# Four graph layers on one core: the head of the last layer reordered, and two small reorderings in its skip LSTMs

## The chip, the cores and the metric

The kernel runs on one core of one Trainium2 chip. The metric is the time of one execution on the device in microseconds (us), and the median of the runs is compared. The core has five engines, each with its own in-order instruction queue: TensorE (PE, matmuls; its weight loads are shown apart as PEld), VectorE (DVE), ScalarE (ACT), GpSimd (POOL), and SyncE (SP), which here only starts DMA transfers. An instruction waits at the head of its queue until the semaphores that it names have been reached, and all behind it wait too.

## What is computed

The input `x` is 128 sequences of 64 positions with 256 features; a graph of 64 nodes connects the positions. Four layers follow each other, each of the form `x = layernorm(x + layer(x))`. The change lies wholly in the last one:

```
h = relu(adj @ (x @ Wg0 + bg0))
h = relu(adj @ (h @ Wg1 + bg1))
for p in 1..4:                       # skip LSTMs
    nw = 64 // p                     # windows of p positions
    last = LSTM_p(windows of h)      # p steps, gates i, f, g, o; zero start; last hidden state
    h[:, p-1, 2p-1, ...] = last      # written over the last position of each window
x = layernorm(x + h)
```

All of it is in float32. The third layer ends with a batch norm over all rows, so nothing of the last layer's input exists before the third layer is complete.

## The kernel before

**Blocks, groups, pairs.** The rows are cut into 16 blocks of 512 (8 sequences). Two blocks make a group of 16 sequences, two groups a pair. There are four pairs, and the LSTMs run pair after pair (`lstm(pair)`), with both groups of a pair side by side in tiles such as `H[:, group, k]`, the input of the LSTMs (features on the partitions, `k` or `m` is the half of the 256 features).

**The graph convolutions, `gcn`.** It is a generator, one block each, and is advanced one step at a time. For the first four blocks the steps are:

1. start two loads of the residual `x2r` (L964); scale the third layer's result by the batch norm (four ACT operations, L970);
2. and 3. for each half `a`: four PE transposes (L988), then `norm`: the residual sum (L994), statistics (L95, L96, L85, L98) on DVE, the power and the normalisation on POOL (L86, L100), and two stores of the result (L999);
4. `neighbours`: the 64 small matmuls with the graph (L953), whose two result banks are copied into `hT` or `xs` by DVE (L1019) and ACT (L1020);
5. and 6. the first weight matrix for each half `m` of the features (L1026), the bias on DVE (L1028), the relu on ACT (L1030);
7. and 8. the second weight matrix for each half `a` of the rows (L1038), its bias on DVE (L1041);
9. `neighbours` again, and the relu into `H` by DVE (L1049) and ACT (L1050).

Blocks 0 and 2 take their PSUM banks from the pool `g` (two banks), blocks 1 and 3 from the pool `l` (six banks), which the LSTMs use as well. Blocks 0 and 1 fill group 0 of pair 0 and blocks 2 and 3 group 1.

**The head of the layer.** Before the LSTMs of pair 0 can start, blocks 0 and 1 must be through. A list of block numbers written out by hand, `for n in [0, 0, 0, 1, 1, 1, ...]`, says in which order the steps of the four blocks are issued; the steps that are left of blocks 2 and 3 are put beside the first units of the LSTMs with `put(pair, part, unit, ...)`.

**What fixes the order.** Each step is recorded through `given`, which puts it behind the latest recorded instruction of every engine. So the order of the list is the order of every engine's queue; within one step a scheduler may still move independent instructions past each other.

**The LSTMs.** For p=1 a window is one position: `gates` issues the three gates of a quarter (L1075, six matmuls of 512 columns per unit), and DVE writes the result back into `H` (L1086). For p=2 to 4 the first step of the windows has no hidden state: `plain` issues its gates from `H` (L1183), with two groups `g` and two halves `k` for each half `m`. Later steps (`Gate`, L1218) use seven products in place of eight. After the last step of a window, `output` writes `o * tanh(c)` (L1148) in four parts, one for each half `m` and group, back into `H`, from which the next p starts; for p=4 it writes into `lasts` instead (tile `hd`, L1139). The write of half 0 of group 0 comes first, those of half 1 of group 1, half 0 of group 1 and half 1 of group 0 follow.

**The end.** The last thing in the program is `final` of the last two groups with `pieces=2`, group 1 ahead of group 0: `hd` is transposed on PE (L1363), added to the residual (L1364), normalised, and stored (L1368).

Of the kernel before, what the change touches and what calls it, by code (L numbers as in the profile page):

```python
# [34 lines left out]
SKIP = 4  # L35
# [6 lines left out]
def kernel(ctx: ExitStack, tc: tile.TileContext, i, out):  # L42
# [72 lines left out]
    with ExitStack() as two:  # L115
# [598 lines left out]
        def hidden(q, m):  # L714
            return Z[q][:, m, :] if m < 2 else Aq(q)[:, (m - 2) * QT:(m - 1) * QT]
# [16 lines left out]
        def put(q, m, p_):  # L732
            nc.scalar.activation(hidden(q, m), p_, AF.Identity, bias=b1[:, m:m + 1])
# [112 lines left out]
    def lbank(shape):  # L846
        return ps.tile([P] + shape, F32, name="l", bufs=6)
# [4 lines left out]
    def given(do, *args):  # L852
        traced = nc.cur_bb.bb.instructions
        first = len(traced)
        with ExitStack() as order:
            for e in latest.values():
                order.enter_context(tc.issue_after(e))
            r = do(*args)
        for t in traced[first:]:
            if t.engine in (mybir.EngineType.PE, mybir.EngineType.DVE, mybir.EngineType.Activation,  # L860
                            mybir.EngineType.Pool):
                latest[t.engine] = t
        return r
# [189 lines left out]
    def gate_of(n):  # L1053
        return "ifgo".index(n), AF.Tanh if n == "g" else AF.Sigmoid

    def lstm(pair):
# [36 lines left out]
        for p in range(2, SKIP + 1):  # L1093
# [9 lines left out]
            def inp(r, s, m):  # L1103

                w0 = runs[r][0] * p
                return H[:, :, m, w0:w0 + nw * p, :].rearrange("p n (w s) b -> p n w s b", s=p)[:, :, :, s, :]

            def rows():
                return [late.tile([P, 2, nw, GB], F32, name="gate", bufs=6) for m in range(2)]
# [21 lines left out]
            def output(r, s, m, o, t, groups):  # L1131

                last = s == p - 1
                if last and p == SKIP:
                    for n in groups:

                        if (pair * 2 + n) not in lasts:
                            lasts[pair * 2 + n] = late.tile([P, 2, KD, P], F32, name="hd", bufs=3)
                        nc.vector.tensor_mul(lasts[pair * 2 + n][:, :, m],  # L1139
                                             *(v[m][:, n].rearrange("p (c w) b -> p c (w b)", c=2) for v in (o, t)))  # L1140
                    return

                dst = inp(r, s, m) if last else hid[:, m]
                if len(groups) == 2:
                    nc.vector.tensor_mul(dst, o[m], t[m])  # L1145
                else:
                    n = groups[0]
                    nc.vector.tensor_mul(dst[:, n], o[m][:, n], t[m][:, n])  # L1148

            def bias_of(n, m):  # L1150
                at, f = gate_of(n)
                return f, bias[:, p - 1, 2 * at + m:2 * at + m + 1]
# [15 lines left out]
            def tanh(n, tiles, m):  # L1168
                if n == "i":
                    nc.scalar.activation(tiles["g"][m], cell[:, m], AF.Tanh)  # L1170

            def plain(n, r, tiles):

                t = tiles[n] = rows()
                at, _ = gate_of(n)
                for m in (1, 0):
                    f, b = bias_of(n, m)
                    joint = 2 * nw * GB <= QT
                    banks = lbank([2, nw, GB]) if joint else None
                    for g in (1, 0):  # L1180
                        one = banks[:, g] if joint else lbank([nw, GB])
                        for k in range(KD):
                            nc.tensor.matmul(one, w.raw[0][:, k, at, m, :], inp(r, 0, k)[:, g],  # L1183
                                             start=k == 0, stop=k == KD - 1)
                        if not joint:
                            nc.scalar.activation(t[m][:, g], one, f, bias=b)
                    if joint:
                        nc.scalar.activation(t[m], banks, f, bias=b)
                for m in (1, 0):
                    finish(n, r, 0, tiles, m)  # L1190
                    tanh(n, tiles, m)
# [69 lines left out]
            for r in range(len(runs)):  # L1261
                if p > 2:
                    yield "gap", unit
                for s in range(p):
                    last = s == p - 1
                    if s == 0:
                        tiles = {}
                        for at, n in enumerate("gio"):
                            if at == 0 and p > 2:
                                given(input_sums, r, 1)  # L1270
                            given(plain, n, r, tiles)
                            if at == 0 and p == 2:
                                given(input_sums, r, 1)
                            if at < 2:
                                yield "at", unit
                                unit += 1
                    else:
                        names = "fgio"
                        for at, n in enumerate(names):
                            G = nxt or Gate(n, r, s, tiles)  # L1280
                            nxt = None
                            G.product(1)
                            G.product(5)
                            if prev:
                                prev.act(1)
                                prev.act(0)
                                prev.after(1)
                                G.product(2)
                                prev.after(0)
                                prev.tanh(1)  # L1290
                            G.product(6)
                            if n == "o":
                                G.act(0, 0)
                            if prev:
                                prev.tanh(0)
                            G.product(7)
                            if at == 0:
                                given(input_sums, r, s + 1)
                                G.product(3)
                                G.product(2)  # L1300
                                G.product(4)
                            elif at < 3:
                                G.product(4)
                                G.product(3)
                            if at < 3:
                                yield "at", unit
                                unit += 1
                            prev = G
                        o = prev
                        prev = None  # L1310
                        o.act(1, 1)
                        o.product(3)
                        o.act(0, 1)
                        o.product(4)
                        o.act(1, 0)
                        given(output, r, s, 0, o.tiles["o"], o.tiles["g"], (0,))

                    if not last:
                        tiles = {}
                        nxt = Gate("f", r, s + 1, tiles)  # L1320
                        for j in (1, 5, 6, 7, 3, 2):
                            given(nxt.part, j, 0)
                    elif p < SKIP:
                        yield "wait", unit + 1
                    if s:
                        given(output, r, s, 1, o.tiles["o"], o.tiles["g"], (1,))
                        given(output, r, s, 0, o.tiles["o"], o.tiles["g"], (1,))
                        given(hidden_sums, s, lambda: output(r, s, 1, o.tiles["o"], o.tiles["g"], (0,)))
                    else:
                        given(hidden_sums, s, lambda: None)  # L1330
                    yield "at", unit
                    unit += 1
                    if not last:
                        yield "gap", unit
# [38 lines left out]

    parts = [gcn(n // 2, n % 2, gbank if n % 2 == 0 else lbank, "hT" if n % 2 == 0 else "xs") for n in range(4)]
    first = [prepare(weights_of[0, p]) for p in (2, 3)]
    for n in [0, 0, 0, 1, 1, 1, 0, 1, 0, 1, 2, 0, 1, 2, 0, 1, 3, 2, 0, 1, 0, 1, 3, 2, 3]:
        given(next, parts[n])
    for part in first:
        next(part)
# [7 lines left out]
            kind, u = key if isinstance(key, tuple) else ("at", key)  # L1387
            side.setdefault((pair, kind, u), []).append(part)

    put(0, parts[2], 0, 0, 1, 1)  # L1390
    put(0, parts[3], 0, 1, 1, 2, 2)
    put(0, parts[2], 2)
    put(0, parts[3], 2)
    put(0, first[0], 3, 4)
    put(0, first[1], 9, 11)

# [6 lines left out]
    for k in range(NP):  # L1403
# [5 lines left out]
        for n in range(2):  # L1409
            g = k * 2 + n  # L1410
            for s in range(SKIP - 1):
                u = 34 + 4 * s + 2 * n
# [59 lines left out]
```

## Time and profile before

| | |
|---|---|
| median of 3 runs | 2073.12 us (2072.30, 2073.12, 2073.14) |
| the profiled execution | 2071.63 us, of which 2069.8 us are the span of the engines' records |
| granted TensorE clock over the span | 0.985 |
| PE busy | 1970.3 us (95%) in 11619 matmul passes |
| DVE / ACT / POOL busy | 56% / 46% / 35% |
| the last layer | from about 773 us to the end |

A float32 matmul stands in the records as two passes. A line of the chain or of the timeline gives the start in us, the length, the engine, the program's line, the operation, `output<-inputs`, the shape and a count. In brackets stands how long the engine had been idle before it and what ended that. A row of the windows view gives, for one stretch, the busy time of each engine, the granted clock of PE as a share of full speed, and the busy share of the DMA engines.

### The profile page before, as it was taken

To read this page: it belongs to the slowest core of one execution; us is meant where nothing else is said; L and a number is where in the kernel's file an instruction comes from. 1 tells how busy PE (TensorE), PEld (TensorE's weight loads), DVE (VectorE), ACT (ScalarE), POOL (GpSimd) and SP (SyncE) were. 2 spreads that over 40 slices of the span, in tenths; PEclk is the share of its full clock that TensorE was granted. 3 is DMA by queue.
4 is the path that set the end of the run, shared out by engine and by line. 5 is a ranking of instruction groups with operands and counts; after the bars stand their busy time and mean duration, and the time that the engine had idled before them with its cause. 6 is when DMAs were issued, how large, how long until landed. Compare 5 with 4: busy or idle time off the path is not lost.

```text
span 2069.8 us, 31352 instructions
## 1 busy us (share of the span) xinstructions
PE 1970.3 (95%) x11619; PEld 1379.4 (67%) x11619; DVE 1161.1 (56%) x2643; ACT 955.8 (46%) x1835; POOL 720.2 (35%) x890
## 2 busy tenths in 40 slices
PE   5999999998899999999999999999999999999997
PEld 4666667675454446587688587678587678586675
DVE  7456665554544446564566664566674466443556
ACT  2766666665337403543333643333644343533333
POOL 1123343343210004363445253245253245133354
PEclk9999999999999999999999999999999999999999
DMA  5354343332201128351232622032521031301012
GB/s 143 69 69 66 74 78 54 55 54 44 45 32 19 41 86 282 96 178 51 93 132 69 202 91 87 11 138 64 195 73 77 1 128 62 127 1 77 1 61 72
DMA packets 235961, 170.68 MB, mean 82 GB/s; under 512 B 150560, under 2 KB 213536, under 8 KB 232480
## 3 DMA queue, kind: packets, MB, share of 16 engines
q1 hardware_dynamic: 233952, 166.72, 28.8%
q8 instruction: 91, 1.49, 0.3%
q0 software_dynamic: 1024, 1.05, 0.2%
q10 hardware_dynamic: 832, 0.92, 0.1%
q14 instruction: 62, 0.51, 0.1%
HBM read 107.82 MB, written 60.82 MB: 81 GB/s over the span
## 4 chain that ended last, share of the span: by engine, by line
PE 75%; DVE 14%; ACT 4%; POOL 3%; issue 3%; DMA 1%; SPq 0%; DVEq 0%; POOLq 0%; ACTq 0%
PE l L1218 26%; PE l L1183 9%; PE l L1075 8%; PE pz L789 5%; PE pz L727 5%; PE e L331 3%; PE m L303 3%; PE g L1038 2%; PE m L238 2%; PE m L306 2%; PE z L340 2%; PE m L421 1%; DVE cell L1162 1%; PE g L953 1%; DVE ln_st L95 1%
## 5 line engine op out<-in xcount | busy, mean ns | idle before, releaser
L1218 PE MATMUL l<-xs,wx 128*128 128x256 f32 (+1 forms) x896 | 276.8, 399 | 5.1 <-DVE gate L1237 4.1
L1218 PE MATMUL l<-hs,wh 128*128 128x256 f32 (+1 forms) x896 | 275.1, 399 | 3.1 <-DVE hs L1112 3.1
L1233 ACT ACTIVATE kept<-l 128x256 f32<-128x256 f32 (+1 forms) x224 | 88.4, 402 | 340.0 <-PE l L1218 338.8
L86 POOL TENSOR_TENSOR ln_rs<-ln_rs,mhalf 128x2 f32<-128x2 f32 (+2 forms) x98 | 83.3, 850 | 454.0 <-DVE ln_rs L98 442.6
L1218 PE MATMUL l<-H,wx 128*128 128x256 f32 (+1 forms) x672 | 210.2, 401 | 3.4 <-DVE gate L1246 3.4
L1218 PE MATMUL l<-hid,wh 128*128 128x256 f32 (+1 forms) x672 | 208.8, 399 | 0.0
L1218 PEld LDWEIGHTS l<-xs,wx 128*128 128x128 f32 x896 | 168.8, 190 | 49.4 <-POOL st L100 5.1
L1218 PEld LDWEIGHTS l<-hs,wh 128*128 128x128 f32 x896 | 169.3, 190 | 45.5 <-DVE hs L1112 5.7
L1183 PE MATMUL l<-H,wx 128*128 128x256 f32 (+1 forms) x768 | 190.0, 407 | 10.1 <-DVE H L1148 10.1
L1251 ACT ACTIVATE gate<-gate,bias 128x512 f32<-128x512 f32 (+1 forms) x280 | 170.1, 656 | 35.2 <-DVE gate L1242 31.0
L1183 PEld LDWEIGHTS l<-H,wx 128*128 128x128 f32 x768 | 148.5, 195 | 51.7 <-DVE H L1148 16.0
L1075 PE MATMUL l<-H,wih 128*128 128x512 f32 x384 | 166.1, 593 | 0.0
L342 ACT ACTIVATE u<-z 128x1024 f32<-128x1024 f32 x128 | 130.3, 1025 | 64.2 <-PE z L340 63.4
L1218 PEld LDWEIGHTS l<-H,wx 128*128 128x128 f32 x672 | 126.0, 190 | 38.4 <-DVE gate L1246 7.4
L1218 PEld LDWEIGHTS l<-hid,wh 128*128 128x128 f32 x672 | 127.2, 190 | 32.0 <-issue 2.6
L1075 PEld LDWEIGHTS l<-H,wih 128*128 128x128 f32 x384 | 72.7, 190 | 89.3 <-issue 83.0
L1241 POOL TENSOR_TENSOR gate<-gate,kept 128x256 f32<-128x256 f32 (+1 forms) x84 | 65.0, 774 | 159.2 <-DVE kept L1239 159.2
L314 DVE TENSOR_TENSOR qs<-m,qs 64x256 fp32r<-64x256 f32 x128 | 54.0, 422 | 109.5 <-ACT qs L313 107.3
L727 PE MATMUL pz<-A,w 128*128 128x512 f32 x256 | 113.1, 595 | 0.0
L340 PE MATMUL z<-gath_r,qs 128*128 128x512 f32 x256 | 100.5, 480 | 0.6 <-ACT u L342 0.4
L1116 POOL TENSOR_TENSOR hs<-hid 128x256 f32<-128x256 f32 (+1 forms) x28 | 25.8, 921 | 207.0 <-DVE hid L1145 123.3
L1170 ACT ACTIVATE gate<-cell 128x512 f32<-128x512 f32 (+1 forms) x88 | 58.6, 666 | 82.4 <-DVE cell L1162 58.8
(277 smaller groups left out, 3629.2 us busy)
## 6 DMA issues: line engine op xcount, KB each, us to landing
wx<-sums SPq DMA_DIRECT2D x9, 2048.0 KB
wh<-sums SPq DMA_DIRECT2D x9, 1792.0 KB
way<-st SPq DMA_DIRECT2D x54, 256.0 KB
st<-way SPq DMA_DIRECT2D x216, 64.0 KB
xin<-in_x SPq DMA_DIRECT2D x16, 512.0 KB
ld<-table SPq DMA_DIRECT2D x16, 512.0 KB
x_dram<-y SPq DMA_DIRECT2D x16, 512.0 KB
x2r<-x_dram SPq DMA_DIRECT2D x32, 256.0 KB
```

The lines of the kernel that those rows point to most:

```text
L86: nc.gpsimd.tensor_tensor(dst, dst, mhalf[:, :n], OP.pow)
L303: nc.tensor.matmul(pq, xT[:, k, c * P:(c + 1) * P], wq[:, k, :], start=k == 0, stop=k == KD - 1)
L340: nc.tensor.matmul(z[:, k, :], L1[q]["qs"][c][:, s, k * P:(k + 1) * P], gath_r, start=True, stop=True)
L342: nc.scalar.activation(u, z, AF.Relu)
L727: nc.tensor.matmul(p_, w1[:, k, m * P:(m + 1) * P], Aq(q)[:, k * QT:(k + 1) * QT], start=k == 0, stop=k == KD - 1)
L789: nc.tensor.matmul(p_, w2[:, k, m * P:(m + 1) * P], hidden(q, k), start=k == 0, stop=k == M1 - 1)
L1075: nc.tensor.matmul(b, wih1[:, k, mw * P:(mw + 1) * P], Hw[:, k], start=k == 0, stop=k == KD - 1)
L1183: nc.tensor.matmul(one, w.raw[0][:, k, at, m, :], inp(r, 0, k)[:, g], start=k == 0, stop=k == KD - 1)
L1218: nc.tensor.matmul(self.banks[j], lhs, rhs, start=src == 0, stop=src == 1)
L1233: nc.scalar.activation(self.keep(j), b, AF.Copy)
L1241: e.tensor_tensor(t[0][:, 1], t[0][:, 1], k[5], OP.add)
L1251: given(lambda: nc.scalar.activation(dst, dst, f, bias=b))
```

## The change

There are three edits:

- **The head's list is another one, and so are the steps put beside the LSTM's first units.** The first weight matrix of block 0 is now issued between the transposes and norms of block 1, and block 0's second matrix beside block 1's first. Both norms of block 2 stand ahead of block 1's last step; block 2's first `neighbours` has left the head for unit 0 of the LSTMs. Beside the units, the remaining steps of blocks 2 and 3 take turns.
- **In `plain` group 0 is issued ahead of group 1.**
- **For the last step of p=4 alone, the four writes into `hd` come in another order:** half 1 of group 1 is moved up, ahead of the last gate's product 4 and so of its DVE sum (L1244), and half 0 of group 0 is moved behind half 0 of group 1.

```diff
--- before.py
+++ after.py
@@ plain @@
-                    for g in (1, 0):
+                    for g in range(2):
                         one = banks[:, g] if joint else lbank([nw, GB])
@@ last step of a window @@
                         o.act(0, 1)
+                        if p == SKIP and last:
+                            given(output, r, s, 1, o.tiles["o"], o.tiles["g"], (1,))
                         o.product(4)
                         o.act(1, 0)
-                        given(output, r, s, 0, o.tiles["o"], o.tiles["g"], (0,))
+                        if p < SKIP or not last:
+                            given(output, r, s, 0, o.tiles["o"], o.tiles["g"], (0,))
...
                     if s:
-                        given(output, r, s, 1, o.tiles["o"], o.tiles["g"], (1,))
+                        if p < SKIP or not last:
+                            given(output, r, s, 1, o.tiles["o"], o.tiles["g"], (1,))
                         given(output, r, s, 0, o.tiles["o"], o.tiles["g"], (1,))
+                        if p == SKIP and last:
+                            given(output, r, s, 0, o.tiles["o"], o.tiles["g"], (0,))
                         given(hidden_sums, s, lambda: output(r, s, 1, o.tiles["o"], o.tiles["g"], (0,)))
@@ head @@
-    for n in [0, 0, 0, 1, 1, 1, 0, 1, 0, 1, 2, 0, 1, 2, 0, 1, 3, 2, 0, 1, 0, 1, 3, 2, 3]:
+    for n in [0, 0, 0, 1, 0, 1, 0, 1, 0, 1, 0, 1, 2, 0, 1, 0, 1, 3, 1, 2, 2, 1, 3, 3]:
         given(next, parts[n])
...
-    put(0, parts[2], 0, 0, 1, 1)
-    put(0, parts[3], 0, 1, 1, 2, 2)
-    put(0, parts[2], 2)
-    put(0, parts[3], 2)
+    for n, u in [(2, 0), (3, 0), (2, 1), (2, 1), (3, 1), (3, 1), (2, 2), (2, 2), (3, 2), (3, 2), (2, 2), (3, 2)]:
+        put(0, parts[n], u)
```

The number of instructions on each engine stays the same. The order of POOL's queue does not change at all. On SP's queue seven transfers at the head trade places: block 2's second residual load and a load of `wh` go ahead of block 1's stores, two loads of `z` for later blocks and two residual loads of `final` go ahead of block 2's stores, and a third load of `z` goes behind the two stores of the weight sums.

## The prediction

> **What bounds the kernel now.** I read the page first, then the chain of waits, then the timeline and windows of the three places that are edited.
>
> ```profile
> PE 1970.3 (95%) x11619; PEld 1379.4 (67%) x11619; DVE 1161.1 (56%) x2643; ACT 955.8 (46%) x1835; POOL 720.2 (35%) x890
> L1183 PE MATMUL l<-H,wx 128*128 128x256 f32 (+1 forms) x768 | 190.0, 407 | 10.1 <-DVE H L1148 10.1
> ```
>
> PE is the bound. No edit changes its passes, so only PE's idle time and its clock can move the end. `plain` (L1183) waits 10.1 us in all for the writes of `H`, at the changes from p=2 to 3 and 3 to 4 of four pairs. The head has more:
>
> ```profile
> 776.00:780.00 4.00, 2.81 (x12) 2.41 (x12) 2.66 (x10) 1.83 (x4) 0.70 (x1) 0.57 0.99 315
> 783.00:789.00 6.00, 4.46 (x94) 3.24 (x85) 3.47 (x11) 1.19 (x2) 3.74 (x7) 0.50 0.75 219
> 790.00:808.00 18.00, 18.00 (x255) 13.18 (x254) 12.03 (x27) 8.77 (x15) 3.57 (x6) 1.00 0.85 290
> 808.00:866.00 58.00, 58.00 (x337) 29.93 (x336) 28.10 (x56) 29.30 (x47) 19.95 (x22) 1.00 0.43 153
> ```
>
> Until 789 us PE has gaps and half a clock (0.50); from 790 to 866 it is busy without a gap at full clock. So what the head's edit does before 790 must also survive to 866. The steps there:
>
> ```profile
> 782.69 1.24 PE L953 MATMUL g<-bdT,A 64*64 64x64 f32 x32 [0.78 <-POOL A L100]
> 785.16 0.68 DVE L1019 COPY hT<-g 128x512 f32<-128x512 f32 x1
> 787.85 2.94 PE L1026 MATMUL g<-hT,wg 128*128 128x512 f32 x4
> 805.80 1.06 DVE L1049 TENSOR_SCALAR H<-l 128x512 f32<-128x512 f32 x1
> 807.85 5.32 PE L1075 MATMUL l<-H,wih 128*128 128x512 f32 x12
> ```
>
> Block 0's graph matmuls end at 783.93, but its copy stands on DVE behind block 1's norms (785.16). The LSTM's first unit starts at 807.85.
>
> The other two places, at a change of p with other work beside it, at the same change in the last pair, and at the end:
>
> ```profile
> 1036.60 1.33 DVE L1148 TENSOR_TENSOR H<-gate 128x336 f32<-128x336 f32 x3
> 1037.57 3.72 PE L1183 MATMUL l<-H,wx 128*128 128x256 f32 x16 [0.73 <-DVE H L1148]
> 1961.24 5.06 PE L1183 MATMUL l<-H,wx 128*128 128x256 f32 x11 [3.57 <-DVE H L1148]
> 1961.00:1967.00 6.00, 5.75 (x14) 4.59 (x15) 0.61 (x2) 0.69 (x1) 3.67 (x6) 0.50 0.01 3
> 2056.80 0.41 DVE L1244 TENSOR_TENSOR gate<-l,kept 128x256 f32<-128x256 f32 x1
> 2057.13 1.42 DVE L1139 TENSOR_TENSOR hd<-gate 128x256 f32<-128x256 f32 x4
> 2058.27 0.66 PE L1363 MATMUL g<-ident,hd 128*128 128x128 f32 x4 [3.66 <-DVE hd L1139]
> ```
>
> [...] The trace agrees: its record of the granted clock has stretches of 3.41 and 6.83 us at half, and one grid of 3.413 us windows fits them; windows filled to 46% or less were followed by half clock (one with 41% was not)[...]. [...]
>
> **The head.** I laid out the steps on each engine in its order, with these durations: a norm 1.98 us of DVE and 1.9 us more until POOL has stored it (777.30, 779.18, 781.17 in the timeline); copy or bias 0.70; write of `H` 1.05; relu 0.62; passes 0.43 (L1026), 0.215 (L1038), 0.107 (L988), twice that at half clock. For the order before this gives 807.81 for the first L1075, where the trace has 807.85. For the new order, with the trace's clock windows:
>
> - Block 0's copy is on DVE at 783.7 and its L1026 starts at 784.5, 3.3 us earlier. That is the gain.
> - DVE now holds that copy, and the bias of block 0's first half, ahead of block 1's norms. They run at 784.6 and 788.5 (before 781.17 and 783.17); block 1's graph matmuls end at 792.6 in place of 787.9. PE stands 1.9 us for them, as block 0's second matrix is queued behind.
> - After that PE has 14.0 us of work before L1075 (8 passes L1026, 32 L1038, 128 L953, 16 L988), 0.4 us of wait for a relu, and possibly 1.7 us from a window at half clock. Through at 809.4.
> - But the write of `H` of block 1 (L1049) now stands on DVE behind both norms of block 2: bias at 806.8 to 807.5, norms to 811.4, write to 812.5. PE idles 3.2 us; L1075 starts at 812.6: **+4.8**.
> - Block 2's graph matmuls (64 passes, 0.99 us) are still to be done then: **+1.0**.
> - The 3.2 us gap costs a further window at half clock as a rule: **+1.7**.
>
> That is +7.5 for the profiled windows. Moved over a whole period of the windows, the same layout gives +3.0 to +7.5, mean **+5.7**. From there to 866 PE is as full as before: the regrouped steps beside units 0 to 2 have the same passes, and each unit's 12 passes (5.2 us) cover the copies and biases that they wait for. SP's trades cost nothing: block 2's residual is issued near 783 and read at 807, block 3's near 793 and read at 812 (before 787.60 and 806.69), under the first norms; `wh` is read by POOL at 818 and `z` by ACT at 841. POOL's order is the same, its weight sums (813 to 824 now) end 5 us later and are needed near 866. Were a residual late, the start of L1075 would be later by that, at most 2 us.
>
> **`plain`.** With group 1 first, its first matmul needs the third write of `H`. With group 0 first it needs the first write; the built order then has one (p=3) or two (p=4) matmuls ahead of the one that needs the fourth write. So PE fills its wait:
> - 2 to 3, three pairs with side work: PE is free at 949.76, started at 950.12, now has no wait: -0.36 each.
> - 3 to 4, three pairs: before, eight matmuls of 0.43 from 1037.57 end at 1041.0. Now two in 1036.84 to 1037.70, the fourth write ends at 1037.94, six more end at 1040.6: -0.45 each.
> - Last pair: starts at 1875.61 for 1876.28 (-0.67) and 1960.40 for 1961.24 (-0.84), the ends of the first writes.
> - Sum -3.9. PE is nearly gapless after each change, so it is carried on. Bounds: -2.0 if half is lost again to the gates of the first recurrent step, -3.9.
> - The last pair's gaps shrink from 3.2 to 2.5 and from 3.56 to 2.7 us, which shortens the half clock after them: mean over the windows -1.2, between 0 and -3.1.
>
> **The writes into `hd`.** At 2056.80 DVE would wait for ACT's half 1 (to 2057.09), then L1244, then half 0 of group 1 as third, which ends at 2058.22, as before: the same start for PE. L1244 comes 0.66 later and with it the last ACT piece and the fourth write; the residual sum (L1364, 2058.75) is behind it: +0.1 (0 to +0.3). In the first three pairs PE goes on with 41 us of L1075, which hides it; the bank that L1244 frees is taken again six allocations later, 4 us on.
>
> **Sum.** +5.7 - 3.9 - 1.2 + 0.1 = **+0.7**. Against the profiled execution (2071.63, whose windows lay well at the head: 0.7 us below the mean of my layout) the same sum with its own windows is +7.5 - 3.9 - 2.8 + 0.1 = +0.9. The median shown is 1.5 us above it; means go on the median: 2073.1 + 0.7 = 2073.8. A measurement of this kernel tells about 0.2% (4.1 us) from no change.
>
> **Rivals.**
> - *No change to be told (0.65)*: the two cancel; own range 2070.5 to 2077.3.
> - *Slower: the head's DVE order wins (0.27).* L1049 behind two norms keeps +7.5 and the gain of `plain` is half lost (-2.0, -0.4 of clock): +5.2, 2078.3. For it: the gap is a matter of order, while the gain must survive 90 us of recurrent steps with DVE waits. It decides from a loss in the head of 4.1 above what `plain` returns. A late residual would add up to 2.
> - *Faster (0.08)*: the gap happens to lie across two windows and leaves the clock alone (+3.0), the last pair keeps full clock (-3.1) and all of -3.9 is carried: -3.9, 2069.2, the edge of 0.2%. It needs lucky windows in most runs.
> - *The head's reordering does what its order says at first sight*, 3.3 us earlier throughout: then -3.3 - 5.0, 2064.8. Against it stands DVE's order; it has 0.03 of the 0.08.
>
> The range leaves out the ends of the last three: 2069.5 to 2079.0.
>
> **What would show it.** Right: first L1026 near 784.7; block 1's last L953 of step 4 near 792.6; first L1075 at 811 to 812.6, idle for about 3 us until L1049; L1183's wait for L1148 down from 10.1 to about 6; first L1363 as long after L1246 as before. Wrong: L1075 starting before 809 without a gap, or L1218 showing new waits for L1112 after the changes of p.

## The result: no difference that can be measured, and two parts that cancel

The changed kernel takes 2073.24 us (median of 12 runs, 2070.33 to 2075.00), the kernel before 2073.13 us beside it (12 runs, 2071.16 to 2075.17). The ratio is 0.9999, with a 95% interval from 0.9991 to 1.0008. The profiled execution took 2070.33 us (span 2068.6), that of before 2071.63 us. It is the fastest of the twelve, so what its trace gives in sum can lie a few us off the medians.

The page of the changed kernel, first the engines' busy time, then the group of `plain` (busy time and mean ns of one, then the idle time before it and what ended it):

```profile
PE 1970.3 (95%) x11619; PEld 1378.4 (67%) x11619; DVE 1163.3 (56%) x2643; ACT 956.0 (46%) x1835; POOL 722.2 (35%) x890
L1183 PE MATMUL l<-H,wx 128*128 128x256 f32 (+1 forms) x768 | 187.9, 403 | 6.1 <-DVE H L1148 6.1
```

PE is as busy as before, to the digit. Its wait ahead of L1183 has gone from 10.1 to 6.1 us. So 4 us of waiting were won there, and the medians show no gain: something was lost somewhere else. The timeline of the changed kernel at the head:

```profile
784.54 2.85 PE L1026 MATMUL g<-hT,wg 128*128 128x512 f32 x4
791.42 0.99 PE L953 MATMUL l<-bdT,A 64*64 64x64 f32 x32 [1.25 <-POOL A L100]
808.75 1.00 DVE L1049 TENSOR_SCALAR H<-l 128x512 f32<-128x512 f32 x1
809.85 7.08 PE L1075 MATMUL l<-H,wih 128*128 128x512 f32 x12 [2.62 <-issue]
```

Block 0's first matrix is 3.3 us earlier than before (784.54). But the LSTM's first unit is 2.0 us later (809.85 for 807.85), after a gap of 2.62 us. The name behind the arrow, "issue", says only that the profile has no semaphore for this wait. The line above it points to the cause, which e4 below tries: the write of `H` by L1049 starts at 808.75 and ends at 809.75, behind the two norms of block 2 that the new list put ahead of it on DVE (they start at 804.88). The graph matmuls that it reads had ended at 806.20, and ACT's half of the same step (L1050) started at 806.30. The 12 passes then take 7.08 us, where they took 5.32 before. The windows view of the same stretch shows half clock behind the gap (length, busy us of PE, PEld, DVE, ACT, POOL, granted clock, DMA):

```profile
790.00:808.00 18.00, 15.91 (x228) 11.89 (x220) 9.39 (x19) 8.91 (x15) 2.82 (x5) 1.00 0.67 242
806.90:810.30 3.40, 0.78 (x5) 0.39 (x3) 3.29 (x10) 1.74 (x2) 3.08 (x6) 0.99 0.27 87
810.20:813.60 3.40, 3.40 (x5) 1.35 (x4) 3.19 (x14) 0.34 (x1) 2.38 (x6) 0.51 0.78 230
840.00:866.00 26.00, 26.00 (x192) 13.78 (x192) 13.26 (x24) 13.82 (x23) 1.41 (x2) 1.00 0.13 41
```

In the 3.4 us that hold the gap PE was busy for 0.78, and the next 3.4 us ran at half clock. From 840 to 866 PE is full, so nothing of the loss comes back. In the LSTMs, at the changes of p (in pair 0 from 2 to 3 and from 3 to 4, then both in the last pair):

```profile
954.29 8.15 PE L1183 MATMUL l<-H,wx 128*128 128x336 f32 x28
...
1042.14 6.31 PE L1183 MATMUL l<-H,wx 128*128 128x256 f32 x28 [0.29 <-DVE H L1148]
...
1877.58 12.80 PE L1183 MATMUL l<-H,wx 128*128 128x336 f32 x38 [2.53 <-DVE H L1148]
...
1960.64 9.65 PE L1183 MATMUL l<-H,wx 128*128 128x256 f32 x36 [2.73 <-DVE H L1148]
```

The waits of 0.36 and 0.73 us beside other work have become none and 0.29, those of the last pair 2.53 and 2.73 us (3.20 and 3.57 before).

**The ledger.** I compared the start of the same PE instruction in both traces, counted from the first L922 (an offset of 0.24 us). After minus before, in us:

| place on PE | after - before | step |
|---|---|---|
| first L1026 | -3.07 | |
| first L1075 | +2.24 | |
| end of the head (first L1183 of pair 0) | +4.94 | **+4.94** |
| pairs 0 to 2, each: p 2 to 3, and 3 to 4 | -0.56, -0.44 | **-3.0** in all |
| pair 0, p=4 | | +0.30 |
| last pair, p 2 to 3, and 3 to 4 | -1.73, -2.26 | **-3.99** |
| from the last L1218 to the first transpose of `hd` | | +0.49 |
| first transpose of `hd` | -1.30 | sum -1.26, rest rounding |

The step at the head is 2.24, another 1.7 of half clock, and 1.0 for block 2's graph matmuls, which now come after. The sum, -1.3 us, is that of two single executions; the medians differ by +0.1.

### The profile page after: what moved, and what is told of

Its sections match the earlier page's. It is cut to its first block, busy times and chain, and to the rows that moved or that the text cites. A ratio compares the mean times of both kernels' runs of the same rounds, so it can differ in the third digit from the quotient of the medians.

```text
span 2068.6 us, 31355 instructions
## 1 busy us (share of the span) xinstructions
PE 1970.3 (95%) x11619; PEld 1378.4 (67%) x11619; DVE 1163.3 (56%) x2643; ACT 956.0 (46%) x1835; POOL 722.2 (35%) x890
## 4 chain that ended last, share of the span: by engine, by line
PE 76%; DVE 14%; POOL 3%; ACT 3%; issue 3%; DMA 1%; SPq 0%; DVEq 0%; POOLq 0%; ACTq 0%
PE l L1218 27%; PE l L1183 9%; PE l L1075 8%; PE pz L789 5%; PE pz L727 5%; PE e L331 3%; PE m L303 3%; PE g L1038 2%; PE m L306 2%; PE z L340 2%; PE m L238 1%; PE g L953 1%; PE g L1026 1%; DVE ln_st L95 1%; PE m L421 1%
## 5 line engine op out<-in xcount | busy, mean ns | idle before, releaser
L1218 PE MATMUL l<-xs,wx 128*128 128x256 f32 (+1 forms) x896 | 276.8, 399 | 5.3 <-DVE gate L1237 4.3
L1218 PE MATMUL l<-hs,wh 128*128 128x256 f32 (+1 forms) x896 | 275.1, 399 | 3.1 <-DVE hs L1112 3.1
L1218 PE MATMUL l<-H,wx 128*128 128x256 f32 (+1 forms) x672 | 210.2, 401 | 3.4 <-DVE gate L1246 3.4
L1218 PE MATMUL l<-hid,wh 128*128 128x256 f32 (+1 forms) x672 | 208.8, 399 | 0.0
L1218 PEld LDWEIGHTS l<-xs,wx 128*128 128x128 f32 x896 | 168.8, 190 | 49.7 <-POOL st L100 5.4
L1218 PEld LDWEIGHTS l<-hs,wh 128*128 128x128 f32 x896 | 169.3, 190 | 45.5 <-DVE hs L1112 5.7
L1183 PE MATMUL l<-H,wx 128*128 128x256 f32 (+1 forms) x768 | 187.9, 403 | 6.1 <-DVE H L1148 6.1
L1183 PEld LDWEIGHTS l<-H,wx 128*128 128x128 f32 x768 | 146.7, 193 | 46.4 <-DVE H L1148 10.4
L1075 PE MATMUL l<-H,wih 128*128 128x512 f32 x384 | 167.9, 598 | 2.6 <-issue 2.6
L1218 PEld LDWEIGHTS l<-H,wx 128*128 128x128 f32 x672 | 126.0, 190 | 38.4 <-DVE gate L1246 7.4
L1218 PEld LDWEIGHTS l<-hid,wh 128*128 128x128 f32 x672 | 127.2, 190 | 32.0 <-issue 2.6
L1075 PEld LDWEIGHTS l<-H,wih 128*128 128x128 f32 x384 | 73.3, 192 | 93.2 <-issue 86.9
```

The source lines that it names most:

```text
L1075: nc.tensor.matmul(b, wih1[:, k, mw * P:(mw + 1) * P], Hw[:, k], start=k == 0, stop=k == KD - 1)
L1218: nc.tensor.matmul(self.banks[j], lhs, rhs, start=src == 0, stop=src == 1)
```

## The experiments

All times are medians beside runs of the kernel before on the same chip; its median was 2070.7 to 2074.2 us on the chips used, so kernels are compared by their ratio to it. A ledger is that of one execution, whose time can lie up to 5 us off the median of its kernel: e1's trace is of the fastest of its six (2076.17 us), e4's of the slowest of its 21 (2075.44).

### The three edits one by one

The head's list and the steps beside the units, as in the change, and nothing else (e1):

> Only the head's list and the steps beside units 0 to 2 are changed. Theory 1 (two effects cancel): +4.9 us as read from the trace of the changed kernel at the first L1183, +3 to +7.5 by the clock's windows, so about 2078; first L1075 near 810 to 812, idle 2.5 to 3 us ahead of it. Theory 2 (neither edit reaches the end): within 1 us of the kernel before. Theory 3 (the early start of block 0 pays and something later takes it back): -3.

Measured: 2079.81 us, ratio 1.0030 (1.0018 to 1.0042), some 6.2 us slower. Its timeline has the same gap, as long as in the changed kernel:

```profile
806.20 1.09 PE L988 MATMUL l<-ident,A 128*128 128x128 f32 x8
809.91 7.08 PE L1075 MATMUL l<-H,wih 128*128 128x512 f32 x12 [2.62 <-issue]
```

By its ledger it is 5.08 us behind at the end of the head and 4.9 at the end.

`plain` alone (e2):

```diff
-                    for g in (1, 0):
+                    for g in range(2):
```

> Only the order of the groups in plain is changed. Theory 1: -3.9 us from the filled waits and about -1.2 (0 to -3.1) from the clock of the last pair, so about 2068; L1183's wait for L1148 falls from 10.1 to 6.1 us. Theory 2: within 1 us, the time being waited again at the first recurrent step.

Measured: 2066.10 us, ratio 0.9962 (0.9948 to 0.9975), some 7.9 us faster. The three first pairs give 3.0 us in its ledger, as in the changed kernel. The last pair gives 5.7 (3.4 and 2.3).

The order of the writes into `hd` alone (e3):

> Only the order of the writes into hd is changed. Theory 1: 0 to +0.3 us, first L1363 1.80 us after the last L1246 as before. Theory 2 (half 1 of group 1 being early frees group 1's end): -0.4.

Measured: 2073.81 us, ratio 0.9999 (0.9990 to 1.0007). In the changed kernel's timeline the way from DVE's L1246 to the first transpose (now L1369) is 1.80 us, as before (56.47 to 58.27):

```profile
2054.93 0.42 DVE L1246 TENSOR_TENSOR gate<-l,gate 128x256 f32<-128x256 f32 x1
...
2056.73 2.32 PE L1369 MATMUL g<-ident,hd 128*128 128x128 f32 x8 [4.16 <-DVE hd L1139]
```

Together the three are 6.2 - 7.9 - 0.2 = -1.9 us, with a half width of some 4 us; the whole change is -0.2 (-1.9 to +1.7). They add up within that: the change is a loss at the head and a gain in `plain` of nearly the same size.

### Is the loss at the head the place of L1049?

The changed kernel, with block 1's last step (the write of `H`) ahead of block 2's norms (e4); one step of block 3 goes from unit 0 to unit 1:

```diff
-    for n in [0, 0, 0, 1, 0, 1, 0, 1, 0, 1, 0, 1, 2, 0, 1, 0, 1, 3, 1, 2, 2, 1, 3, 3]:
+    for n in [0, 0, 0, 1, 0, 1, 0, 1, 0, 1, 0, 1, 2, 0, 1, 0, 1, 3, 1, 1, 2, 2, 3, 3]:
...
-    for n, u in [(2, 0), (3, 0), (2, 1), (2, 1), (3, 1), (3, 1), (2, 2), (2, 2), (3, 2), (3, 2), (2, 2), (3, 2)]:
+    for n, u in [(2, 0), (2, 1), (2, 1), (3, 1), (3, 1), (3, 1), (2, 2), (2, 2), (3, 2), (3, 2), (2, 2), (3, 2)]:
```

> The changed kernel with block 1's last step (L953, L1049, L1050) put back ahead of block 2's norms in the list, and block 3's first graph matmuls moved from unit 0 to unit 1. If L1049 behind two norms is what costs the head its time (theory 1): the first L1075 comes 2 us earlier than in the changed kernel, with no gap over 1 us ahead of it, and no half clock after it: 3 to 4 us faster than the changed kernel, about 2069.5. If the head's loss is in block 1's late norms instead: as the changed kernel, within 1 us.

Measured: 2070.54 us, ratio 0.9984 (0.9977 to 0.9991): 0.15% (3.1 us) better than the changed kernel's ratio, with a half width of 0.11%; 3 to 4 us had been expected if the place of L1049 is what costs. The first L1075 has no gap ahead of it and is only 0.43 us later than before. But my hand-made order brought a gap of its own in unit 2, and half clock after it:

```profile
821.50 5.84 POOL L902 TENSOR_TENSOR wx<-wx 128x512 f32<-128x512 f32 x4
824.46 1.76 DVE L1086 TENSOR_TENSOR H<-hid,gate 128x512 f32<-128x512 f32 x1
...
830.29 5.40 PE L1026 MATMUL l<-xs,wg 128*128 128x512 f32 x8 [1.99 <-ACT xs L1020]
```

PE waits 1.99 us for the copies of block 3, which stand behind DVE operations that took 1.76 in place of 0.68 us while POOL formed its weight sums. In this trace 5.47 us are lost by the end of the head all the same. It is the slowest execution of the 21, and its last layer already starts 3.7 us later than in the trace of before; how often the gap in unit 2 comes, one trace does not tell. So the order of L1049 makes the gap at 809.85, as the prediction had it, and to take it away was worth some 3 us over the runs, with a new gap in its place in this one.

The next one keeps e4's list, with two of block 3's steps of unit 1 moved to unit 2, `plain` with group 0 first, and the writes of `hd` as before (e5):

> plain with group 0 first, the writes into hd as in the kernel before, and a third head: block 0's convolutions between block 1's norms, block 1's last step ahead of block 2's norms, block 3's first graph matmuls behind block 2's first convolution in unit 1, its two convolutions in unit 2. Theory 1 (the head's loss came from L1049 behind two norms, its half clock, and in e4_write_first from a copy late on DVE in unit 1): as fast as plain alone, 2066 within 1.5 us, no gap over 1 us on PE from 796 to 870 us. If a late block 1 costs time by itself: 2 to 4 us slower than plain alone.

Measured: 2070.33 us as the median of thirteen executions, 2069.80 without one that took 11301 us and that the ratio leaves out; ratio 0.9978 (0.9970 to 0.9987). That is 0.16% (3.3 us) above `plain` alone (half width 0.16%), where the first theory had the two within 1.5 us and the second had 2 to 4 us. PE has no gap from 811 to 850 us, and the ledger is 1.3 us behind e2 at the end of the head (block 2's graph matmuls come after the start). Another 2.8 us are lost later, mostly in the last pair. The windows there, first e2, then e5, on the grid of each run's clock:

```profile
1871.07:1874.48 3.41, 1.62 (x8) 1.09 (x6) 3.24 (x9) 1.81 (x4) 0.00 (x0) 1.00 0.42 86
1874.48:1877.89 3.41, 2.67 (x9) 1.74 (x10) 1.70 (x6) 1.57 (x4) 1.97 (x3) 1.00 0.96 408
```

```profile
1875.59:1879.00 3.41, 1.32 (x4) 0.79 (x5) 3.01 (x9) 1.41 (x4) 0.62 (x1) 1.00 1.02 327
1879.00:1882.41 3.41, 3.41 (x8) 2.05 (x7) 0.00 (x0) 1.08 (x2) 3.00 (x4) 0.50 1.00 427
```

Both kernels have the same gap of 2.53 us. In e2 it lies across two windows, which are 47% and 78% busy, and the clock stays; in e5 more of it falls into one, which is 39% busy, and the next runs at half clock. So a gap of one length was followed by a window at half clock in one of the two traces and not in the other. What put it elsewhere on the grid I did not isolate, and that this is what parts the medians is not shown: the mean granted clock of the runs is 0.984 for both kernels.

### The clock by itself

To take that away, unused matmuls fill the gap. A helper writes a bank that nothing reads; each matmul is two passes of 0.215 us. It also takes a turn of the pool `l`; what that does by itself was not tried.

```diff
+    def warm(n):
+        p_ = lbank([QT])
+        for _ in range(n):
+            nc.tensor.matmul(p_[:, :2 * P], ident, wih1[:, 0, :2 * P], start=True, stop=True)
...
                     elif p < SKIP:
+                        if pair == NP - 1 and r == len(runs) - 1:
+                            given(warm, 5)
                         yield "wait", unit + 1
```

On `plain` alone (e6):

> plain with group 0 first, and five more matmuls of 256 columns (2.15 us at full clock, their result unused) ahead of the last pair's two changes of p. Theory 1 (the idle of PE there halves its clock afterwards): no half clock at 1870 to 1970 us in any window, 1 to 2 us faster than plain alone (2064 to 2065), although PE does more. If the half clock costs nothing there since DVE or ACT set the pace: the same as plain alone or up to 1 us slower.

Measured: 2064.05 us, ratio 0.9953 (0.9939 to 0.9967). In its timeline the matmuls stand in the gap (the trace names them by their first buffer and L1057), the wait is 0.37, and the granted clock is 1.00 from 1876.3 to 1960.4 us:

```profile
1874.33 2.32 PE L1057 MATMUL l<-wih,ident 128*128 128x256 f32 x10
1877.02 13.37 PE L1189 MATMUL l<-H,wx 128*128 128x336 f32 x46 [0.37 <-DVE H L1154]
```

At the head of e1, with `given(warm, 5)` right after the list (e7):

> The new head alone (as e1_head), and five more matmuls of 256 columns (2.15 us, unused) in PE's gap ahead of the first L1075. Theory 1 (the gap has two costs, its own length and the half clock after it): the first L1075 starts where it did, the half clock after it is gone, 1.7 us faster than e1_head, about 2077.5 to 2078. If the clock is not part of the head's cost: as e1_head, 2079 to 2080.

Measured: 2080.33 us, ratio 1.0031 (1.0019 to 1.0043); no gain on e1. At its place the fill did what it should:

```profile
810.47 2.32 PE L1057 MATMUL l<-wih,ident 128*128 128x256 f32 x10
813.31 5.39 PE L1081 MATMUL l<-H,wih 128*128 128x512 f32 x12 [0.51 <-DVE H L1049]
```

The 12 passes took 5.39 in place of 7.08 us, and by the end of the head this trace is 1.1 us ahead of e1's. It then loses 2.0 us at another place, where e1 loses 0.3, at a recurrent step of pair 0:

```profile
1114.00:1117.40 3.40, 1.72 (x7) 0.88 (x6) 3.23 (x9) 1.47 (x4) 0.54 (x1) 1.00 0.45 125
1117.40:1120.80 3.40, 3.40 (x9) 2.67 (x9) 2.62 (x6) 0.67 (x2) 1.37 (x2) 0.50 0.20 65
```

There PE stands in two pieces for DVE's L1237 and L1246, 0.95 and 0.43 us in the trace of before, 1.24 and 0.43 in that of the changed kernel; here both fell into one window, which was idle for 1.68 us. All six runs of e7 have the same granted clock over the span, 0.982, and times within 0.9 us of each other, and the mean of e1's six is 0.982 too. So over the runs the fill took nothing off the half clock in sum, which agrees with this trace: what it saved at the head came back elsewhere. That it came back at this place in each run was not seen.

The fill in the last pair of the whole change (e8), of the kernel before with seven matmuls, as its gaps are longer (e9), and of e5 (e11):

> The changed kernel with five unused matmuls in the two gaps of PE in the last pair (changes of p from 2 to 3 and 3 to 4), which keep those gaps short. What it leaves of the head's edit is then not mixed with the clock of the last pair. Theory 1 (the head's edit costs PE some 5 us by its DVE order and one stretch at half clock, and nothing is lost later): against the kernel with `plain` alone and the same fill (2064.05) it is 4 to 6 us longer, 2068 to 2070, and in its trace there is no half clock between 1000 and 2050 us. Theory 2 (the head's edit costs more than its place shows, as later steps wait too): 2071 or more. Rival (the cost of the head is a matter of where the clock's windows fall, and vanishes with them): 2064 to 2066.

> The kernel before with seven unused matmuls in each of the two gaps of PE in the last pair; nothing else is changed, so `plain` still waits for the third write of `H`. Theory 1 (of the 8 us that the order of groups in `plain` brought, about 4 is filled wait and the other 4 is the clock at these two gaps): the fill alone brings the two stretches at half clock after 1875 and 1960 us, some 3 us each in the profiled run, 2067 to 2069, and what is left of the order of groups is the 4 to 5 us between it and 2064.05. Theory 2 (the fill of the wait is worth it by itself and the clock next to nothing): no change, 2072.5 to 2074.

> `plain` with group 0 first, the head's order with block 1's last step ahead of block 2's norms, and the same five unused matmuls in the two gaps of the last pair. Without them this was 2070.33, 4.2 above `plain` alone, while its trace is only 1.3 behind at the end of the head and loses the rest in the last pair to half clock. Theory 1 (the head in this order costs 1 to 1.5 us and only the clock's windows made it 4): 2065 to 2066. Theory 2 (the head's order costs 4 us by itself): 2068.

| kernel | without fill | with fill |
|---|---|---|
| before | 1 | e9: 2070.16 us, 0.9987 (0.9981 to 0.9994) |
| the change | 0.9999 (0.9991 to 1.0008) | e8: 2068.55 us, 0.9978 (0.9969 to 0.9987) |
| `plain` alone | e2: 0.9962 (0.9948 to 0.9975) | e6: 0.9953 (0.9939 to 0.9967) |
| e5 | 0.9978 (0.9970 to 0.9987) | e11: 2067.30 us, 0.9969 (0.9958 to 0.9980) |

The fill gains 0.13, 0.21, 0.09 and 0.09%, some 2 to 4 us. The first two are clear of the noise (half widths 0.06 and 0.12), the last two are not (0.19 and 0.14). For e9 neither theory had it: less than the 4 to 6 us expected, as the profiled run of before from which I took the price had more half clock in the last pair (13.7 us) than any other trace of this case, and not nothing. With the clock of the last pair out of the way, e8 is 0.25% (5.2 us, half width 3.4) above e6, which is the cost of the head and the `hd` order (4 to 6 expected), and e6 is 0.34% (7.0 us, half width 3.2) below e9. The ledger gives the order of groups 4.0 of these 7 us (3.0 in three pairs, 1.0 in the last); another 1.5 lie at the head, where the two traces differ in their half clock and no edit differs, and 1.5 at the end. e11 is 3.3 us above e6 (half width 3.7), where 1 to 2 were expected if the clock had made the difference and 4 if this order of the head costs time by itself, so the runs leave that open; its trace is 1.1 us behind e6 at the end of the head and loses another 2.0 in pair 0 at the same place as e7, with half clock from 1111 us.

### A faster version

e6, with unused matmuls in the gaps of the head too (e10): 28 of 128 columns ahead of the first matmul of the layer, 12 ahead of block 0's graph matmuls, 3 ahead of block 1's.

> The kernel with `plain` alone and the fill in the last pair (2064.05), and now unused matmuls in three gaps of the head as well: 28 of 128 columns ahead of the first one of the last layer, 12 of 256 ahead of block 0's graph matmuls, 3 between them and block 1's. Theory 1 (PE's first steps of the head run at half clock because of the gaps between 773 and 789 us, and its 8 transposes, last 32 graph matmuls and first 4 passes of L1026 would take 1.0, 0.6 and 1.3 us less at full clock): the stretch at half clock from 775 to 792 is gone and the time is 2061 to 2063. Theory 2 (the head is paced by the norms on DVE, 2 us each, and filling gaps only shifts): 2063.5 to 2065. If the fill stands ahead of work that was ready, it is longer: 2066.

Measured: 2062.96 us, ratio 0.9951 (0.9937 to 0.9964). The stretch at half clock is gone, and the four passes of block 0's first matrix take 1.98 us, where they took 3.22 in e6:

```profile
771.78 6.42 PE L923 MATMUL g<-bdT,ident 128*128 128x128 f32 x56
...
789.43 1.98 PE L1028 MATMUL g<-hT,wg 128*128 128x512 f32 x4
```

From the end of the layer before to that row it is 17.5 us, in e6 17.2: the fill is too long, since the transposes could start at about 776.7. With 20 in place of 28 (e12):

> The kernel with fill in the head as well (2062.96), with 20 in place of 28 unused matmuls ahead of the first one of the last layer. In its trace the 28 (two passes each, 6.4 us) ended at 778.0, while ACT had the first scaled tiles from about 776.7, so they held the transposes up by some 1.5 us. Theory 1 (the head is now paced from the transposes on, by the norms): the first L1075 comes 1.5 us earlier after the last matmul of the layer before and the time is 2061.0 to 2062.0; the clock stays full, since the gap that comes back is under 1 us. Theory 2 (with the shorter fill the clock is halved again at the head): 2063.5 to 2065.

Measured: 2062.56 us, ratio 0.9959 (0.9946 to 0.9973). The clock stayed up (the four passes of block 0's first matrix take 1.98 us again, the granted clock over the span is 0.990) and the transposes came 1.7 us earlier, but block 0's first matrix did not (789.53): the first norm now waits for its residual's transfer, and the norms seem to pace what follows. The first L1075 did not come 1.5 us earlier than in e10, as expected, but 0.9 us later (37.4 us from the end of the layer before, in e10 36.5).

```profile
779.22 0.69 DVE L996 TENSOR_TENSOR x2r<-g,x2r 128x512 f32<-128x512 f32 x1 [1.86 <-DMA x2r<-x_dram]
```

e6, e10 and e12 can't be told apart, and all three beat both kernels by 0.4 to 0.5%: the order of groups in `plain` and a fill, without the head's new list. Nor can they be told from e2, which has no fill (0.9962; e6 is 0.09% below it, half width 0.19%). So the gain that is shown is that of the order of groups.

## Why the prediction was right, and where its sizes were off

- **The outcome.** 2073.8 us and "no change" as the likeliest were right, and for the reason given: a loss at the head against a gain in `plain`. e1 and e2 show the two sides; the interval of neither holds 1. That the median came within 0.6 us of the forecast is luck: the single terms were off by up to 3 us.
- **The head.** First L1026 near 784.7 (784.54), block 1's last graph matmul near 792.6 (792.4), a wait for L1049 behind block 2's norms: each came. The sum was too large: +7.5 for the profiled windows, +4.94 in the trace. The step that failed is "possibly 1.7 us from a window at half clock. Through at 809.4." The clock was back at 786.3 and stayed until 810.2, so PE was through at 807.2 and DVE's norms started 2.6 us earlier than laid out. The terms given for 809.4 also come to 808.7 only (792.6 + 14.0 + 0.4 + 1.7); 0.7 us of it stand in no term. The other terms held: a gap of 2.62 for 3.2, 1.0 for block 2, 1.7 for the window after the gap. The mean of +5.7 over the windows is inside the measured +6.2 (3.7 to 8.7) of e1. No residual of blocks 2 and 3 came late. "Until 789 us half a clock" was read too broadly: in the trace of before the clock is full from 779.6 to 783.0.
- **`plain`, the waits.** Forecast -3.9: -0.36 and -0.45 in each of three pairs, -0.67 and -0.84 in the last. The ledger has -0.56, -0.44, and the gaps shrank by 0.67 and 0.84. The 0.2 us more at p=3 are behind the gap that I read; what ran shorter there I did not isolate. The bound of -2.0 was not needed, since all was carried. The +0.30 in pair 0 belongs to the head's list: e1 has it without `plain` (+0.30), e2 does not (+0.02), and PE's wait for DVE's L1237 there is 1.24 us in e1 and the changed kernel, 0.95 before and 0.96 in e2.
- **`plain`, the clock.** -1.2 as a mean, -2.8 for the profiled windows. In the trace the last pair gave 3.99, of which 1.51 are the gaps; the rest, 2.5, I put to the clock (13.7 us of half clock before, 6.8 after). As a mean it was probably too small: e2 measured 7.9 (5.2 to 10.8), and waits and clock together had been put at 5.1, just outside the interval. The waits explain 0.6 of the difference by the ledger. For the rest the runs speak for the clock: its mean over the span is 0.9842 in e2's five and 0.9823 in the 34 of before beside them. The 0.0019 between them, over 2070 us, are worth up to 3.9 us of PE's work (an estimate from these figures, for a PE that is never short of work), where 1.2 had been put down and some 3.4 are needed.
- **The writes of `hd`.** +0.1 forecast; the distance stayed at 1.80 us, and e3 shows no difference. The +0.49 in the ledger is ahead of L1246. DVE's sum of the other group's end waited 1.01 us for a transfer (0.51 before), and its queue was late to the end by about that; the transfer did not come earlier with the rest. It does not come of the order of the writes: e3 and e8 have the same order, wait 0.44 and 0.48 us there, and their ledgers change by -0.1 and 0.0 on the same way.

```profile
2048.07 0.69 DVE L1364 TENSOR_TENSOR x3r<-st,x3r 128x512 f32<-128x512 f32 x1 [1.01 <-DMA st<-way]
```

The same sum in e8:

```profile
2044.70 0.69 DVE L1372 TENSOR_TENSOR x3r<-st,x3r 128x512 f32<-128x512 f32 x1 [0.48 <-DMA st<-way]
```

- **The rivals.** "Slower, the head's DVE order wins" had the right mechanism, but needed half of the gain of `plain` to be lost, and no part of it was. "3.3 us earlier throughout" holds up to the first L1026 and no further. New waits of L1218 for L1112 were named as a sign of being wrong: they are 3.1 us in both kernels.

## What to carry to other kernels

A step that is moved to the front of one engine's queue is worth what the last step of the stage gains, not the first (here 3.3 us gained at the first L1026, 2.0 us lost at the first L1075): follow every in-order queue to the end of the stage, and see what now stands behind what was moved. Where PE is the bound and has gaps like those of 2.5 to 3.6 us here, price them twice, as idle time and as the half clock that may follow, and measure over several runs, since the second price was not the same each time (a gap of 2.53 us was followed by 3.4 us at half clock in e5 and by none in e2). A few unused matmuls kept the clock up at the gaps they filled in these traces. They did not make the runs agree better (e9's 21 runs spread from 2067.5 to 2073.8 us), and half clock could come back at another place (e7), so look at the clock of the whole span and not at that of the gap alone.

## What was not expected of the hardware

**How full a window was, and the clock after it.** In the trace of before and in that of the changed kernel every change of the granted clock lies on one grid of 3.413 us (to 0.02 us over the whole span), and the stretches at half clock between 769 and 2050 us are 3.41 to 13.65 us long. A window of that grid that was followed by half clock need not have been idle: in e5 one was 39% busy, and in e11 (at 1107.7 us) and e7 (at 1114.0) they were 49 and 51% busy by the modelled ends; one with 47% in e2 was not followed by it. In the traces of before and of the changed kernel, from 769 us on, each of the nine windows at full clock that were 36% busy or less was followed by half clock, none with 54% or more was, and of two between (both in the trace of before) the one with 42% at 779.58 was and the one with 41% at 769.34 was not. Ahead of the last layer a window 56% busy was followed by half clock (66.20 us, before) and one 57% busy was not (66.13 us, the changed kernel). So these traces show a band and no line. The same holds for the way back: between 769 and 2056 us each of the seven windows at half clock that were 92% busy or more was followed by full clock, none of the five with 70% or less was, and of two with 81% in the trace of before the one at 776.17 was and the one at 1960.6 was not. Short gaps can thus be enough, if they share a window: in e11 those of 1.29 and 0.43 us did, and 3.4 us at half clock followed.

**DVE beside POOL.** In the trace of the kernel before, of two equal L1086 the one beside POOL's L902 took 2.6 times as long as the next one, which started after L902 had ended (1.76 and 0.68 us). In e4 such slowed operations (1.72 to 1.76 us, beside L902) stand ahead of the copies that PE waits 1.99 us for.

```profile
819.92 4.29 POOL L902 TENSOR_TENSOR wh<-wh 128x512 f32<-128x512 f32 x3
...
823.00 1.76 DVE L1086 TENSOR_TENSOR H<-hid,gate 128x512 f32<-128x512 f32 x1
...
824.68 0.68 DVE L1086 TENSOR_TENSOR H<-hs,gate 128x512 f32<-128x512 f32 x1
```
